# Turns in the interleaving of two graph layers on TensorE: hysteresis beside the MLP, and another course

## The chip, the cores and the metric

The kernel runs on one core of a Trainium2 chip. The metric is the device time of the program in microseconds. TensorE is called PE in the profile (its weight loads PEld), VectorE DVE, ScalarE ACT, GpSimd POOL, SyncE SP.

## The reference

Two graph layers follow each other on 16 images of 1024 nodes with 256 features, in float32. Layer 0 is a graph attention with four heads of 64 features; in the inputs the adjacency is 0 or 1, so of its five edge types only one occurs. Layer 1 is a masked self-attention with eight heads of 32 features, and an MLP from 256 to 1024 to 256 features with GELU. A layer norm closes each of them.

```python
# layer 0 (type 1 alone, since adj is 0 or 1)
h = einsum('bnd,hde->bhne', x, W)
weight = leaky_relu(mask * (e_src[i] + e_dst[j]), 0.01)      # e_* = h . a_*
att = softmax(where(adj == 0, -1e9, weight))
out = relu(att @ h + bias) + h                               # per head, then a norm per head
x = layernorm(x + out)
# layer 1
n = layer_norm(x) ; q = k = v = heads of n
attn = softmax(where(adj > 0, q @ k.T / sqrt(32), -inf))
x = x + attn @ v
x = layernorm(x + gelu(layer_norm(x) @ W1 + b1) @ W2 + b2)
```

## The kernel before

All code in question is in `fast_path`; `general_path` runs only when a check of the inputs fails. The program is written out instruction by instruction in Python, and the order in which the Python calls are made is the order on TensorE, ScalarE, VectorE and GpSimd. There is no loop on the device: all 16 images are unrolled.

Two generators issue the heavy work. `layer0()` goes image by image through `prepare` (transposes, projections, the mask) and `attention0`; `layer1()` goes through `attention1` and `mlp` one image behind. Each `yield` ends a step, and gives the step's size in units of estimated TensorE time and what the next step needs.

- An `attention0` step, 1.0 unit, is one pair of key blocks for one head and 512 queries. `products` issues 16 matmuls (32 records, since a float32 matmul shows as two) in array tiles of 128*64 from the weights tile `p0` into the PSUM bank `acc`. `weights` makes the `p0` of the step three later (`AHEAD = 3`, four buffers) with two VectorE instructions. There are 32 such steps in an image. Every 16 of them `spread_factor` puts four 32*128 matmuls between.
- An `attention1` step, 2.5 units, has four row-tiled logit matmuls (`ps`, a ring of four PSUM banks), four exponentials on ScalarE, two mask products on VectorE, and value products in tiles of 128*32 (`po`). There are 32 in an image, and they take 82 to 83 units with their beginning.
- An `mlp` step, 1.75 units, is two hidden blocks of the first product (`first`: `ps<-yT,w_sb`, then GELU on ScalarE), or half of one output block of the second (`second`: `po<-w_sb,hid`). Either way it is 8 records in tiles of 128*128. There are 32 in an image, 56 units.

Besides there are `chains`, generators of the smaller work that follows a step: norms, residuals, transposes. `advance()`, which is called after each step, issues a chain's next part as soon as the planner's clock (`Pace`, a model of engine times) has its inputs ready.

The main loop picks the stream of the next step. `place` holds the image and the units done of each stream. `wanted()` turns layer 1's progress into the place where layer 0 should be, along `COURSE`: `WORK0` is 13 + 2 + 32 = 47 units, `ATTN1` 82, `WORK1` 138. Layer 0 has the turn when it is behind the target. A second rule swaps the two when the chosen stream's inputs come over 0.3 us later by the planner's clock than the other's, within `SLACK` of the target:

```python
    SLACK = 0.06
    COURSE = [(0.0, 1.0), (ATTN1, 1.38), (WORK1 - 14.0, 2.0), (WORK1, 2.0)]
    ...
        which = 0 if streams[0] and (at0 < target or not streams[1]) else 1
        if all(streams):
            late = [when(n) - nc.now() for n in needs]
            other = 1 - which
            allowed = at0 < min(target + SLACK, place[1][0] + 2.05) if other == 0 else at0 > target - SLACK
            if allowed and late[which] > max(late[other], 0.0) + 0.3:
                which = other
```

`COURSE` says that layer 0 of image b+1 is to have 38% of its 47 units done when layer 1's attention of image b ends, and all of them 14 units before the MLP of image b ends.

Of the kernel before, what the change touches and what calls it, by code (L numbers as in the profile page):

```python
# [176 lines left out]
def fast_path(  # L177
# [141 lines left out]
    def at_time(t):  # L319
        return lambda: t  # L320
# [94 lines left out]
    def when(needs):  # L415
        return max([n() if callable(n) else nc.written.get(n.tensor.name, 0.0) for n in needs] + [0.0])
# [18 lines left out]
    def begin(chain, engine, *needs):  # L435
        for n in needs:
            if not callable(n):
                uses(chain, n.tensor.name)
        chains.append([chain, engine, needs])
# [10 lines left out]
    def advance():  # L450
        for _ in range(2):
            for item in list(chains):
                if item in chains and when(item[2]) <= max(nc.now(), nc.free[item[1]]):
                    run(item)
# [4 lines left out]
    def done(chain):  # L459
        return lambda: math.inf if waits(chain) else 0.0  # L460

    def complete(chain):

        for item in list(chains):
            if item[0] is chain:
                while item in chains:
                    run(item)
# [366 lines left out]
    def finish1(o, x1, yT, heads):  # L834


        complete(heads)
        rowwise = [P, BPH, D]
        nc.vector.tensor_add(o, o, x1)
        mv = small.tile([P, BPH, 2], F32, name="mv1")  # L840
        for g in range(BPH):
            statistics(o[:, g, :], mv[:, g, :])
        v = small.tile([P, BPH], F32, name="v1s")
        nc.vector.tensor_scalar(v, mv[:, :, 1], EPS, None, op0=OP.add)
        r = power(v, BPH, "r1")
        nc.vector.tensor_add(x1, x1, o)
        yield "vector", r
        t = minus_mean(mv[:, :, 0], r, BPH)
        yield "scalar", t
        scale_shift(o, o, t, r, BPH)  # L850
        for g in range(0, BPH, GB):
            yield "tensor", o, side_ready
            transpose_rows(yT[:, :, g * P : (g + GB) * P], o[:, g : g + GB, :])

    def add_bias2(x1):
        nc.vector.tensor_add(x1, x1, b2_r[:, None, :].to_broadcast([P, BPH, D]))
        yield from ()

    def in_range(values):

        for op, bound in ((OP.max, LOW), (OP.min, HIGH)):
            seen = small.tile([P, NR], F32, name="seen")
            nc.vector.scalar_tensor_tensor(seen, values, bound, values, op0=op, op1=OP.is_equal)
            nc.vector.tensor_tensor(okr, okr, seen, op=OP.min)
# [78 lines left out]
    def finish_norms(b, n):  # L943
        for chain in [c for at, c in norms.items() if at[:2] == (b, n)]:
            complete(chain)

    place = [[0, 0.0], [0, 0.0]]

    def layer0():
        for b in range(B):  # L950
            place[0][:] = b, 0.0
            seen = three.tile([P, NR], F32, name="ranges")
            rinv1 = seen[:, 0 : NB * H1].rearrange("p (k h) -> p k h", h=H1)
            rinv0 = seen[:, NB * H1 : NB * (H1 + H0)].rearrange("p (k h) -> p k h", h=H0)
            factors = seen[:, NB * (H1 + H0) : NR].rearrange("p (k h) -> p k h", h=H0)
            hb = []
            esr = one.tile([P, N], F32, name="esr")
            dinv = two.tile([P, NB, H0], F32, name="dinv")
            v0 = one.tile([P, NB, H0, HO + 1], F32, name="v0")
            mask = [two.tile([P, NB, HALF], U8, name=f"mask{n}") for n in range(NH)]  # L960
            yield from prepare(b, hb, esr, v0, dinv, mask)
            handed[b] = seen, rinv1, mask
            yield from attention0(b, hb, v0, esr, dinv, factors, mask, rinv0)
        place[0][:] = B, 0.0

    def layer1():
        for b in range(B):
            place[1][:] = b, 0.0
            seen, rinv1, mask = handed.pop(b)

            def half(n):
                if (b, n) not in handed:
                    finish_norms(b, n)
                return handed[b, n]

            yT = [two.tile([P, DC, HALF], F32, name="yT") for _ in range(NH)]
            halves = {}

            def half_done(n, o, heads):
                finish_norms(b, n)  # L980
                x1 = handed[b, n][0]
                chain = finish1(o, x1, yT[n], heads)
                bias = add_bias2(x1)
                halves[n] = x1, yT[n], chain, bias
                begin(chain, "vector", done(heads), o)
                begin(bias, "vector", at_time(nc.now() + 24.0), x1)

            yield from attention1(half, mask, rinv1, half_done)
            complete(weights_of_later)
            yield from mlp(b, halves)  # L990
            in_range(seen)
# [4 lines left out]
    WORK0 = NB // GB * 3.25 + 2.0 + NB * H0 * 1.0  # L996
    ATTN1 = 2.0 + 2.5 * (NH * NB * H1 // QUAD)
    WORK1 = ATTN1 + NB // GB * (1.75 * FC / 2 + 3.5 * GB)
    SLACK = 0.06
    COURSE = [(0.0, 1.0), (ATTN1, 1.38), (WORK1 - 14.0, 2.0), (WORK1, 2.0)]  # L1000

    def wanted():
        b, done = place[1]
        for (start, low), (end, high) in zip(COURSE, COURSE[1:]):
            if done < end:
                return b + low + (high - low) * (done - start) / (end - start)
        return b + COURSE[-1][1]

# [2 lines left out]
    load_blocks(0)  # L1011
    weights_of_later = later_weights()
    begin(weights_of_later, "tensor", at_time(3.0))
    streams, needs = [layer0(), layer1()], [(), ()]
    while any(streams):
        (b0, done0), target = place[0], wanted()
        at0 = b0 + done0 / WORK0
        which = 0 if streams[0] and (at0 < target or not streams[1]) else 1
        if all(streams):
            late = [when(n) - nc.now() for n in needs]  # L1020
            other = 1 - which
# [3 lines that stand above are left out]
        step = next(streams[which], None)  # L1025
        if step is None:
            streams[which], needs[which] = None, ()
        else:
            place[which][1] += step[0]
            needs[which] = step[1:]  # L1030
        advance()
# [393 lines left out]
@with_exitstack  # L1425
def tile_two_graph_layers(ctx: ExitStack, tc: tile.TileContext, *args: bass.AP):
    nc = tc.nc
    pool = ctx.enter_context(tc.tile_pool(name="outcome", bufs=1))
    ok = pool.tile([P, 1], F32, name="ok")
    fast_path(tc, *args, ok)  # L1430
    verdict = pool.tile([1, 1], I32, name="verdict")
    with tc.tile_pool(name="ps_v", bufs=1, space=PSUM) as ps_v, tc.tile_pool(name="sb_v", bufs=1) as sb_v:
        ident = sb_v.tile([P, P], F32, name="ident_v")
        make_identity(nc, ident)
        row = ps_v.tile([1, P], F32, name="row")
        nc.tensor.transpose(row, ok, ident)
        least = sb_v.tile([1, 1], F32, name="least")
        nc.vector.tensor_reduce(least, row, axis=mybir.AxisListType.X, op=OP.min)
        nc.vector.tensor_copy(verdict, least)
    good = nc.values_load(  # L1440
        verdict[0:1, 0:1], min_val=0, max_val=1, skip_runtime_bounds_check_because="it is a product of comparisons"
    )
    with tc.If(good == 0):
        general_path(tc, *args)
# [34 lines left out]
```

## Time and profile before

| what | value |
|---|---|
| time, median of 3 runs | 3568.07 us (3567.42 to 3569.54) |
| the profiled execution | 3565.24 us, its span 3563.4 us |
| granted TensorE clock | 0.974 over the span |
| busy over the span | PE 3446.7, DVE 2984.4, ACT 2010.3, POOL 416.4 us |
| layer 0's products (`acc<-v,p`) | 16384 records, 585.7 us busy, 227 ns each |
| MLP products (`ps<-yT,w_sb` and `po<-w_sb,hid`) | 2048 records each, 487.1 and 490.6 us busy, 386 and 387 ns each |
| one image in the middle of the run | 217.2 us (1847.9 to 2065.1 us) |

Nearly all instructions stand under L61, the line of a helper, so groups are told apart by tile names. The ends of matmuls are modelled and their pipeline overlaps, so for TensorE the difference between the starts of two neighbouring groups says more than the mean duration of one instruction. A line of the timeline merges neighbouring instructions of one form; its count divided by 32 (layer 0's products) or by 8 (the MLP) is a number of steps.

### The profile page before, as it was taken

What the parts mean: (1) busy time and instruction counts of PE and PEld (TensorE: products, weight loads), DVE (VectorE), ACT (ScalarE), POOL (GpSimd) and SP (SyncE); (2) the same over time, 40 slices, a digit from 0 to 9 for tenths busy, and PEclk for the clock granted to TensorE, in tenths of its full rate; (3) what the DMA queues carried; (4) which work ended last, traced back from release to release, by engine and by line L of the source; (5) the groups of instructions that cost most, each with busy time, mean ns of one, the idle gap of its engine ahead of it and who ended that gap; (6) DMA issues with size and microseconds to landing.
All of it is one profiled execution on the core that took longest, in us unless ns stands there. A gap on an engine that the chain in (4) does not pass through costs nothing.

```text
span 3563.4 us, 141495 instructions
## 1 busy us (share of the span) xinstructions
PE 3446.7 (97%) x64417; PEld 2301.0 (65%) x64417; DVE 2984.4 (84%) x5267; ACT 2010.3 (56%) x4320; POOL 416.4 (12%) x424
## 2 busy tenths in 40 slices
PE   6899999999999999999999999999999999999998
PEld 5567576675756658576575766757567585765746
DVE  5898897988879898898988979889798988979873
ACT  2563736547375573846638366473755738466363
POOL 0102011010110101111020110101101011110200
PEclk8899999999999999999999999999999999999999
DMA  4101102011020110201011020110201102010000
GB/s 107 38 15 34 30 13 48 8 36 27 15 48 6 40 21 16 47 12 41 15 32 32 13 45 9 34 30 14 49 6 40 21 15 48 12 37 3 18 4 14
DMA packets 77811, 97.52 MB, mean 27 GB/s; under 512 B 9105, under 2 KB 60049, under 8 KB 77201
## 3 DMA queue, kind: packets, MB, share of 16 engines
q0 software_dynamic: 18432, 33.56, 6.5%
q1 hardware_dynamic: 57184, 53.76, 4.9%
q8 instruction: 506, 8.29, 1.0%
q10 hardware_dynamic: 1584, 1.05, 0.1%
q14 instruction: 105, 0.85, 0.1%
HBM read 105.13 MB, written 16.78 MB: 34 GB/s over the span
## 4 chain that ended last, share of the span: by engine, by line
PE 84%; DVE 8%; ACT 4%; issue 2%; DMA 1%; POOL 0%; POOLq 0%; ACTq 0%; DVEq 0%
PE po L61 32%; PE ps L61 31%; PE acc L61 22%; DVE p L61 7%; ACT p L61 2%; ACT sq L61 1%; DVE x L61 1%; ACT mask L61 1%; ACT z L61 0%; DMA w0e<-in_L_gnn_W_dram 0%; DVE hb L61 0%; ACT oT L61 0%; DMA xl<-in_L_gnn_a_dst_dram 0%; ACT o L61 0%; ACT xT L61 0%
## 5 line engine op out<-in xcount | busy, mean ns | idle before, releaser
L61 ACT ACTIVATE p<-ps 128x512 f32<-128x512 f32 x2048 | 1059.6, 610 | 388.2 <-PE ps L61 388.2
L61 DVE TENSOR_TENSOR p<-p,mask 128x1024 f32<-128x1024 f32 x1024 | 1187.6, 1216 | 13.1 <-ACT p L61 13.1
L61 PE MATMUL ps<-nT 32*128 32x512 f32 x4096 | 715.5, 666 | 1.5 <-ACT p L61 1.5
L61 DVE SCALAR_TENSOR_TENSOR p<-cb,dinv,mask 128x512 f32<-128x512 f32 x1024 | 710.9, 743 | 0.7 <-ACT cb L61 0.7
L61 PEld LDWEIGHTS acc<-v,p 128*64 128x64 f32 x16384 | 525.1, 140 | 129.2 <-issue 68.4
L61 PE MATMUL acc<-v,p 128*64 128x65 f32 x16384 | 585.7, 227 | 19.9 <-DVE p L61 12.3
L61 PEld LDWEIGHTS po<-v,p 128*32 128x32 f32 x32768 | 393.0, 110 | 327.7 <-issue 305.9
L61 ACT ACTIVATE hid<-ps,b_sb 128x256 f32<-128x256 f32 x512 | 242.6, 474 | 632.8 <-PE ps L61 632.8
L61 PE MATMUL po<-p,unit 128*32 128x512 f32 x2048 | 550.6, 612 | 0.0
L61 PE MATMUL po<-p,v 128*32 128x512 f32 x2048 | 550.2, 612 | 0.3 <-issue 0.3
L61 PE MATMUL po<-w_sb,hid 128*128 128x256 f32 x2048 | 490.6, 387 | 0.0
L61 PE MATMUL ps<-yT,w_sb 128*128 128x256 f32 x2048 | 487.1, 386 | 0.0
L61 PEld LDWEIGHTS ps<-yT,w_sb 128*128 128x128 f32 x2048 | 376.6, 190 | 64.7 <-issue 11.4
L61 PEld LDWEIGHTS po<-w_sb,hid 128*128 128x128 f32 x2048 | 375.6, 190 | 65.1 <-issue 11.4
L61 PE MATMUL po<-v,p 128*32 128x33 f32 x32768 | 386.8, 198 | 12.1 <-DVE o L61 10.2
L61 PEld LDWEIGHTS ps<-nT 32*128 32x128 f32 x4096 | 241.9, 190 | 121.5 <-issue 50.6
L61 PEld LDWEIGHTS po<-p,v 128*32 128x32 f32 x2048 | 78.3, 108 | 343.9 <-issue 183.2
L61 DVE TENSOR_TENSOR z<-acc,bias_r 128x256 f32<-128x256 f32 x128 | 54.3, 424 | 249.4 <-ACT hb L61 249.2
L61 POOL TENSOR_TENSOR r<-v,mhalf 128x1 f32<-128x1 f32 (+1 forms) x192 | 156.5, 824 | 775.3 <-DVE v L61 631.0
L61 ACT COPY cb<-ps 128x512 f32<-128x512 f32 x128 | 68.8, 589 | 254.7 <-PE ps L61 254.7
L61 POOL TENSOR_TENSOR r<-v1s,mhalf 128x4 f32<-128x4 f32 x32 | 61.6, 1925 | 1078.2 <-DVE v1s L61 1078.2
L61 POOL DMA_DIRECT2D ak<-in_adj_dram x128 | 69.0, 539 | 917.1 <-PE acc L61 897.5
(109 smaller groups left out, 2989.8 us busy)
## 6 DMA issues: line engine op xcount, KB each, us to landing
ak<-in_adj_dram POOLq DMA_DIRECT2D x128, 256.0 KB, 3.9
xk<-in_x_dram SPq DMA_DIRECT2D x64, 256.0 KB, 2.8
xl<-in_x_dram SPq DMA_DIRECT2D x32, 512.0 KB, 3.9
out_dram<-z SPq DMA_DIRECT2D x128, 128.0 KB, 1.7
w_sb<-in_L_gnn_W_dram SPq DMA_DIRECT2D x2, 1024.0 KB, 6.6
v<-in_L_gnn_a_src_dram SPq DMA_DIRECT2D x2, 320.0 KB, 4.4
v<-in_L_gnn_a_dst_dram ACTq DMA_DIRECT2D x1, 320.0 KB, 7.0
xl<-in_L_gnn_a_dst_dram ACTq DMA_DIRECT2D x1, 320.0 KB, 8.2
```

Source lines behind the costliest of these rows:

```text
L61: return method(*args, **kwargs)
```

## The change

It adds a hysteresis to the rule that picks the stream: while layer 1 is in its MLP, the stream that had the last step is favoured by `STAY` = 0.018 of layer 0's course. `which` is kept from one round to the next for that, and it is the stream that really had the step, after the rule on lateness. The course now asks for 34% of layer 0 instead of 38% at the end of layer 1's attention, and lateness may move the place by 0.08 instead of 0.06.

```diff
-    SLACK = 0.06
-    COURSE = [(0.0, 1.0), (ATTN1, 1.38), (WORK1 - 14.0, 2.0), (WORK1, 2.0)]
+    SLACK = 0.08
+    STAY = 0.018
+    COURSE = [(0.0, 1.0), (ATTN1, 1.34), (WORK1 - 14.0, 2.0), (WORK1, 2.0)]
...
-    streams, needs = [layer0(), layer1()], [(), ()]
+    streams, needs, which = [layer0(), layer1()], [(), ()], 0
...
-        which = 0 if streams[0] and (at0 < target or not streams[1]) else 1
+        stay = 0.0 if place[1][1] < ATTN1 else (STAY if which == 0 else -STAY)
+        which = 0 if streams[0] and (at0 < target + stay or not streams[1]) else 1
```

## The prediction

> **What bounds the kernel now.** I read the page first, then the sums over stretches of one image, then TensorE's timeline in the stretch that the change touches, then what one tile's matmuls wait for. From the page, busy time by engine:
>
> ```profile
> PE 3446.7 (97%) x64417; PEld 2301.0 (65%) x64417; DVE 2984.4 (84%) x5267; ACT 2010.3 (56%) x4320; POOL 416.4 (12%) x424
> ```
>
> TensorE is never free for long, so a gain must come from what its busy time is made of. An image takes about 217 us (one image's last MLP turn starts at 1847.9 us, the next one's at 2065.1). Three stretches of it, TensorE first, VectorE third:
>
> ```profile
> 1721.00:1770.70 49.70, 49.01 (x1346) 27.91 (x1345) 48.97 (x67) 30.45 (x59) 1.94 (x1) 1.00 0.02 4
> 1770.70:1847.90 77.20, 77.20 (x1027) 63.60 (x1025) 65.84 (x145) 26.12 (x54) 14.19 (x11) 1.00 0.05 17
> 1847.90:1860.20 12.30, 12.30 (x62) 10.57 (x60) 10.47 (x25) 4.19 (x7) 3.10 (x3) 1.00 0.12 30
> ```
>
> The first is the end of layer 1's attention with the first steps of the next image's layer 0 attention between; VectorE works 48.97 of 49.70 us there. The second is the MLP with layer 0's attention beside it: TensorE 77.20 of 77.20 us, VectorE 65.84. The third is the end of the MLP alone. The granted clock is 1.00 in all. In the second, layer 0's products never wait (the tile view of `acc`; nothing stands under the third line):
>
> ```profile
> L61 PE MATMUL acc<-v,p x800: 220/222/271, 1776.0 to 1847.7; 128*64 128x65 f32 x160
> its engine sat idle before it (us, times) until:
> who waited for it (us, times):
> ```
>
> So the MLP stretch is bound by TensorE's own instruction stream. TensorE's timeline there (start, duration, tile shape of the array, operands, count), the usual pattern and then the one place with longer turns:
>
> ```profile
> 2000.11 1.15 PE L61 MATMUL acc<-v,p 128*64 128x65 f32 x32
> 2001.19 1.99 PE L61 MATMUL po<-w_sb,hid 128*128 128x256 f32 x8
> 2003.11 1.15 PE L61 MATMUL acc<-v,p 128*64 128x65 f32 x32
> 2004.20 1.99 PE L61 MATMUL po<-w_sb,hid 128*128 128x256 f32 x8
> 2006.12 2.09 PE L61 MATMUL acc<-v,p 128*64 128x65 f32 x64
> 2008.14 1.13 PE L61 MATMUL ps<-esr,spread 32*128 32x512 f32 x4
> ```
>
> ```profile
> 1837.19 3.02 PE L61 MATMUL acc<-v,p 128*64 128x65 f32 x96
> 1840.14 1.99 PE L61 MATMUL po<-w_sb,hid 128*128 128x256 f32 x8
> 1841.97 1.89 PE L61 MATMUL ps<-yT,w_sb 128*128 128x256 f32 x8
> 1843.80 1.15 PE L61 MATMUL acc<-v,p 128*64 128x65 f32 x32
> 1844.88 1.99 PE L61 MATMUL po<-w_sb,hid 128*128 128x256 f32 x8
> ```
>
> One layer 0 step is 32 matmul records, one MLP step 8. Take differences of starts, since the ends are modelled. A lone layer 0 step holds TensorE 1.08 us (2000.11 to 2001.19), two 2.02 (2006.12 to 2008.14), three 2.95 (1837.19 to 1840.14): 0.93 a step, and 0.15 each time the stream comes on. A lone MLP step holds it 1.92 us (2001.19 to 2003.11), two 3.66 (1840.14 to 1843.80): every join saves 0.2. **A pair of changes, there and back, costs 0.35 us.** Counted in the timeline from 1770.7 to 1860.2 us, the MLP's 32 steps stand in 21 turns, 16 of them one after another of a single step, with 25 layer 0 steps in 20 turns between.
>
> [...] 1792.6 to 1813 us of VectorE's timeline show `p` pairs of 1.41 us set between row-wise operations of up to 1.22 us.
>
> **The change, part by part.** No instruction is added or removed, no buffer changes, and each stream keeps its order; only the interleaving moves. The order of TensorE, ACT, DVE and POOL is the order in which the program is written. The DMAs of the moved steps are the loads of `xl` (512 KB, in the norms that follow layer 0's products) and the stores of `z`, on SP, past each other by a few us; landing takes 3.9 and 1.7 us by the page. POOL's adjacency loads belong to layer 0's preparation, beside layer 1's attention. No matmul in the MLP stretch waits for a DMA, so I put nothing on them; were that cover gone, one landing would be the cost.
>
> *STAY.* One layer 0 unit is 1/47 of the course. The old rule takes layer 0 whenever it is behind the target. Now the stream that ran last has 0.018 x 47 = 0.85 units of credit, so a turn ends after the position has crossed a band of 1.7 units. An MLP step moves the target by 1.75 x 0.66/42 x 47 = 1.29 units: a turn takes two MLP steps, sometimes three, and then two or three of layer 0. I stepped both rules by hand with unit steps and without the rule on lateness. Old, from 22 units at 83 of layer 1's: 3 MLP steps, then single ones, 22 turns and 25 layer 0 steps. The trace has 21 and 25 with the same beginning, so the stepping can be trusted. New, from 21 units: 4, then 2 or 3, at the end 9 alone, 11 turns. Ten pairs of changes fall away: 10 x 0.35 = 3.5 us an image. The lateness rule (line 1023) can swap streams inside a turn, now within 0.08. In the trace it altered one place of 21; VectorE will be tighter, so I allow for 1.5 broken turns: **-8.5 x 0.35 = -3.0 us** (ends -3.5 and -2.1).
>
> *COURSE and SLACK.* The last step that lateness allows before the MLP starts was that from 21 units (21/47 = 0.447, under 0.395 + 0.06); now that from 20 (0.426 under 0.356 + 0.08; 0.447 is over it). One layer 0 step of seven leaves layer 1's attention for the MLP, where it costs 0.93 us. What leaves is 1.08 us if TensorE is the bound there. It is only about 0.45 us if the step hid the exponentials: an attention step takes 2.63 us at best (1725.94 to 1728.57) and 3.25 with no filler before the next (1728.57 to 1731.82), against 2.63 + 1.08 with one. And it is 1.41 us if VectorE bounds there, which its 48.97 of 49.70 us speak for. Ends +0.5 and -0.5 us; I take 0.
>
> *Work that gets between.* In the stretch four groups of transposes or factor spreads stand where the streams change over, which costs little. With turns of two and two to three, some two of five step borders lie inside a layer 0 turn: 4 x 0.4 x 0.35 = **+0.55 us** (ends 0 and 1.4).
>
> *A new wait.* A turn of three asks for three `p` pairs in 2.8 us, and VectorE makes one in 1.41. The cover is the three pairs made ahead (AHEAD) in four buffers; they fill while two MLP steps run (3.66 us). Behind a late pair on TensorE stands all of both streams, and then VectorE's own norms. VectorE idles 7.8 us of the 77.2 (summed gaps in the trace). The stretch loses about 2.5 us and gains 1.4 of work, so some 4 us of slack are left. The trace has no such turns in number, so bounds: nothing, or 0.35 us in each of 10 turns, 3.5 us. I take **+0.6**.
>
> Sum: -3.0 + 0 + 0.55 + 0.6 = -1.85 us an image. Fifteen images have a partner (15 closing MLP turns; the last MLP runs alone, and the first layer 0 too): **-28 us**. The profiled execution took 3565.24 us (span 3563.4): 3537 for it. The median of the three runs is 2.8 us above it: 3540 us.
>
> **Rivals.** (a) Everything falls away and nothing waits: 15 x (3.5 + 0.2 - 0.3) = 51 us, 3517. For it: the acc view without a wait. Against: VectorE's load. Chance 0.2.
> (b) Lateness breaks the turns, so that the change hardly does what it says: the planner's own VectorE is nearly full too, a third `p` of a turn is seen 0.3 us late, and the stream swaps. Two or three pairs saved are eaten by the other terms: 3560 to 3570. The 16 single steps in a row without a swap speak against it. Chance 0.1.
> (c) Slower: VectorE becomes the bound of the MLP stretch. If a turn starts with one pair ready, its second and third step each wait 1.41 - 0.93 = 0.48 us; in half of ten turns that is 4.8 us an image against 2.4 saved: +2.4 x 15 = +36 us, 3604. It decides from 0.24 us of wait per turn. For it: 92% of the stretch is VectorE's once the saving is made[...]. Against: the turn of three at 1837.19 ran in 2.95 us without a wait. Chance 0.1.
>
> **How the numbers follow.** The forecast has 0.6, and spans -45 to -12 us. A measurement here tells about 0.2%, 7 us, from no change. Faster: 0.6 + 0.2 and a little of (b), 0.82; same: most of (b), 0.08; slower: (c), 0.10. The range 3512 to 3562 holds the forecast and (a) and leaves out (c) and the greater part of (b).
>
> **What would show it.** Right: in the MLP stretch 8-record groups come as 16 or 24 and 32-record groups as 64 or 96, about 11 to 13 MLP turns an image; a lone closing turn of up to nine; an image of about 215.3 us; the stretch still without waits of `acc`; `acc` and MLP matmuls of the same mean duration. Wrong: waits "PE acc <- DVE p" of tens of us (12.3 us in the whole run now) would mean (c); more than 17 turns an image would mean (b); a longer stretch 1721 to 1770.7 would put the fault in the course, not in the turns.

## The result, and the profile after

The changed kernel takes 3509.26 us (median of four runs, 3502.05 to 3519.75) against 3568.81 for the kernel before: ratio 0.9835, interval 0.9808 to 0.9862. A second series gave 3501.26 against 3567.57, ratio 0.9813 (0.9799 to 0.9826). It is faster by 59 to 66 us. The forecast was faster by 28, and 3509 lies just below its range of 3512 to 3562.

The page after, first line of busy time, and the core's span with its mean granted clock, before and after:

```profile
PE 3388.7 (97%) x64417; PEld 2288.7 (65%) x64417; DVE 2983.8 (85%) x5267; ACT 2005.7 (57%) x4320; POOL 424.0 (12%) x424
```

```profile
core 0: 3563.4 us, clock 0.974
```

```profile
core 0: 3510.3 us, clock 0.981
```

TensorE has as many matmuls as before, and VectorE and ScalarE work as long; TensorE is busy 58 us less. The second pair of lines holds what the prediction did not look at. (1 - 0.974) x 3563.4 is 93 us that the clock took away before, (1 - 0.981) x 3510.3 only 67 after.

Two stretches of one image follow: the whole MLP, and the opening of layer 1's attention up to its first value products. The columns are PE, PEld, DVE, ACT and POOL busy with counts, the granted clock and the DMA. First before, then after:

```profile
1770.70:1860.17 89.47, 89.47 (x1083) 74.15 (x1081) 76.29 (x170) 30.31 (x61) 17.29 (x14) 1.00 0.06 19
1860.17:1875.77 15.60, 13.31 (x65) 6.92 (x64) 11.03 (x29) 13.85 (x31) 3.58 (x5) 0.81 0.40 88
```

```profile
1742.90:1831.57 88.67, 88.67 (x1126) 76.11 (x1125) 76.03 (x166) 31.78 (x64) 17.78 (x14) 1.00 0.09 23
1831.57:1844.74 13.17, 11.38 (x58) 5.71 (x57) 10.89 (x31) 12.01 (x32) 3.59 (x5) 0.87 0.33 80
```

The whole MLP, where the turns are, is only 0.8 us shorter, with a 26th layer 0 step and two pieces of the next image's preparation in it. The opening of this image is 2.4 us shorter; ScalarE is busy for 89 and 91% of it, and the clock stands at 0.81 and 0.87. The forecast did not look at this place.

The turns themselves look as forecast (TensorE's timeline after; 96 records are three layer 0 steps, 16 two MLP steps):

```profile
1776.40 3.02 PE L61 MATMUL acc<-v,p 128*64 128x65 f32 x96
1779.35 1.99 PE L61 MATMUL ps<-yT,w_sb 128*128 128x256 f32 x8
1781.18 3.62 PE L61 MATMUL po<-w_sb,hid 128*128 128x256 f32 x16
1784.73 2.09 PE L61 MATMUL acc<-v,p 128*64 128x65 f32 x64
1786.75 1.13 PE L61 MATMUL ps<-esr,spread 32*128 32x512 f32 x4
1787.80 1.15 PE L61 MATMUL acc<-v,p 128*64 128x65 f32 x32
```

Three layer 0 steps still hold TensorE 2.95 us, and the last three lines show a factor spread that now splits a turn of layer 0. In every image the MLP stands in 12 turns instead of 21, and the streams change over 22 times instead of 40; 11 to 13 turns were forecast. The wait for `p`, from the waits of TensorE after, is what it was over the whole run:

```profile
PE acc L61 <- DVE p L61: 12.3, 8, 3.1
```

What did not stand in the prediction is the end of the MLP (timeline of TensorE, before and after):

```profile
1853.17 7.07 PE L61 MATMUL po<-w_sb,hid 128*128 128x256 f32 x32
1860.17 1.14 PE L61 MATMUL ps<-nT 32*128 32x512 f32 x8
1861.24 0.66 PE L61 MATMUL acc<-ident,xk 128*128 128x128 f32 x4
```

```profile
1820.76 1.15 PE L61 MATMUL acc<-v,p 128*64 128x65 f32 x32
1821.85 0.66 PE L61 MATMUL ps<-ident,xk 128*128 128x128 f32 x4
1822.34 0.61 PE L61 MATMUL acc<-identb,ak 128*128 128x128 bf16 x8
1822.79 1.95 PE L61 MATMUL ps<-yT,w_sb 128*128 128x256 f32 x8
1824.57 7.07 PE L61 MATMUL po<-w_sb,hid 128*128 128x256 f32 x32
1831.57 1.14 PE L61 MATMUL ps<-nT 32*128 32x512 f32 x8
```

After layer 0's last step of the image now stand the first two pieces of the next image's preparation: the transposes of x (`xk`) and those of one mask block (`ak`). Before, they came after the first logits of the attention (`ps<-nT`), at 1861.24 us. The rule that the diff adds does this: layer 0 has just had its turn, so its credit of 0.018 is added, and its place 2.0 is below 2.0 + 0.018. The two pieces are 0.95 units, 0.020 of the course, and then the place is past it. I call them the pulled pieces.

### The profile page after: what moved, and what is told of

The parts are those of the page before. It is cut to its first block, busy times and chain, and to the rows that moved or that the text cites. A ratio compares the mean times of both kernels' runs of the same rounds, so it can differ in the third digit from the quotient of the medians.

```text
span 3510.3 us, 141526 instructions
## 1 busy us (share of the span) xinstructions
PE 3388.7 (97%) x64417; PEld 2288.7 (65%) x64417; DVE 2983.8 (85%) x5267; ACT 2005.7 (57%) x4320; POOL 424.0 (12%) x424
## 4 chain that ended last, share of the span: by engine, by line
PE 83%; DVE 9%; ACT 6%; issue 2%; DMA 0%; POOL 0%; ACTq 0%; POOLq 0%; DVEq 0%
PE po L61 32%; PE ps L61 30%; PE acc L61 20%; DVE p L61 7%; ACT p L61 2%; ACT sq L61 1%; DVE x L61 1%; ACT mask L61 1%; ACT hb L61 0%; ACT oT L61 0%; ACT z L61 0%; DMA w0e<-in_L_gnn_W_dram 0%; DVE hb L61 0%; DVE z L61 0%; ACT v L61 0%
## 5 line engine op out<-in xcount | busy, mean ns | idle before, releaser
L61 PE MATMUL ps<-nT 32*128 32x512 f32 x4096 | 698.7, 653 | 0.9 <-ACT p L61 0.7
L61 PEld LDWEIGHTS acc<-v,p 128*64 128x64 f32 x16384 | 514.6, 140 | 99.6 <-issue 48.8
L61 PE MATMUL acc<-v,p 128*64 128x65 f32 x16384 | 558.8, 226 | 19.4 <-DVE p L61 12.3
L61 PE MATMUL po<-w_sb,hid 128*128 128x256 f32 x2048 | 465.9, 381 | 0.0
L61 PEld LDWEIGHTS po<-w_sb,hid 128*128 128x128 f32 x2048 | 387.1, 190 | 63.3 <-issue 11.4
L61 PEld LDWEIGHTS ps<-nT 32*128 32x128 f32 x4096 | 233.4, 187 | 120.9 <-issue 44.8
L61 POOL TENSOR_TENSOR r<-v,mhalf 128x1 f32<-128x1 f32 (+1 forms) x192 | 163.8, 861 | 564.1 <-DVE v L61 529.3
L61 PE MATMUL acc<-w0e,xT 128*128 128x264 f32 x512 | 157.8, 433 | 37.7 <-DVE z L61 22.6
L61 POOL TENSOR_TENSOR r<-v0s,mhalf 128x8 f32<-128x8 f32 x64 | 129.1, 2017 | 526.4 <-DVE v0s L61 526.4
```

Of the source, the lines that this page charges most:

```text
L61: return method(*args, **kwargs)
```

## The experiments

Each run is against the kernel before in the same series (medians 3567.57, 3567.0, 3566.59 and 3569.06 us). "Lost clock" is span times one minus the mean granted clock, median over a kernel's runs. The stretches are means over 14 images of the one profiled execution, read from the trace: MLP; opening, from here on from the first logits to the seventh group of value products, some 36 us; what the clock took from the opening; rest of the attention. The profiled execution is seldom the median one: that of `no_pull` and that of `after_again` are 21 us apart, the medians 32.

| kernel | time | ratio (interval) | lost clock | MLP | opening | its lost clock | rest |
|---|---|---|---|---|---|---|---|
| before | 3567.6 | | 89 | 89.4 | 36.9 | 4.0 | 90.6 |
| course_only | 3562.5 | 0.9986 (0.9979, 0.9992) | 89 | 90.6 | 37.2 | 4.3 | 89.0 |
| no_pull | 3533.3 | 0.9894 (0.9876, 0.9912) | 74 | 87.7 | 37.3 | 3.0 | 89.5 |
| pull_first | 3522.7 | 0.9883 (0.9866, 0.9900) | 74 | 88.1 | 36.6 | 2.7 | 88.8 |
| after_again | 3501.3 | 0.9813 (0.9799, 0.9826) | 60 | 88.6 | 35.6 | 2.7 | 88.9 |
| pull_only | 3548.7 | 0.9950 (0.9936, 0.9964) | 64 | 90.3 | 35.4 | 2.3 | 90.1 |
| stay_only | 3564.9 | 0.9997 (0.9989, 1.0004) | 96 | 89.2 | 37.2 | 3.9 | 90.0 |
| stay_cap | 3510.2 | 0.9834 (0.9820, 0.9847) | 60 | 87.9 | 35.4 | 2.4 | 90.1 |
| act_light | 3477.6 | 0.9749 (0.9736, 0.9762) | 35 | 87.7 | 34.1 | 0.6 | 89.4 |
| sq_dve | 3501.4 | 0.9814 (0.9800, 0.9827) | 60 | 88.6 | 34.9 | 1.8 | 89.0 |
| pull_more | 3525.7 | 0.9881 (0.9864, 0.9899) | 74 | 90.0 | 35.6 | 3.0 | 88.7 |
| pull_far | 3584.6 | 1.0053 (1.0040, 1.0067) | 93 | 99.2 | 30.6 | 4.8 | 88.7 |
| stay_long | 3603.0 | 1.0099 (1.0084, 1.0115) | 104 | 86.6 | 43.8 | 4.8 | 88.9 |
| early | 3645.0 | 1.0220 (1.0206, 1.0234) | 98 | 103.0 | 33.9 | 0.0 | 85.1 |
| long_early | 3644.0 | 1.0215 (1.0201, 1.0229) | 109 | 103.0 | 33.9 | 0.0 | 85.1 |
| slack06 | 3690.2 | 1.0342 (1.0328, 1.0357) | 136 | 104.9 | 35.0 | 1.7 | 85.1 |
| early_hold | 3565.1 | 0.9993 (0.9985, 1.0002) | 43 | 97.4 | 34.5 | 0.7 | 85.0 |

**Taking the change apart.** `no_pull` keeps turns and course, and keeps the pulled pieces out:

```diff
-        stay = 0.0 if place[1][1] < ATTN1 else (STAY if which == 0 else -STAY)
+        stay = 0.0 if place[1][1] < ATTN1 or at0 > place[1][0] + 1.99 else (STAY if which == 0 else -STAY)
```

> The changed kernel, but the credit STAY no longer counts once layer 0 has finished its image, so that the next image's first transposes (x and mask of block 0) stay out of the end of the MLP. Turns and course stay as in the changed kernel (13 MLP turns, 26 layer 0 steps beside the MLP). Theory P (the unforeseen half of the gain comes from these two pieces being pulled into the MLP[...]): lost clock rises from 68 us to about 90 us, the time to 3533 (3525 to 3545) us. Rival T (the whole gain comes from the turns and the moved step): 3509, within 8 us. Rival L[...]: lost clock scatters, no steady difference to the changed kernel.

3533.3 us, as theory P said. Its lost clock did not rise to 90 but to 74, so clock alone is not the link.

`pull_only` is the kernel before with the pulled pieces alone (`STAY` is 0.018, and `which` is kept, as in the change):

```diff
-        which = 0 if streams[0] and (at0 < target or not streams[1]) else 1
+        stay = STAY if place[1][1] >= ATTN1 and which == 0 and at0 > place[1][0] + 1.99 else 0.0
+        which = 0 if streams[0] and (at0 < target + stay or not streams[1]) else 1
```

> The kernel before, with its course, slack and single turns (21 MLP turns, 25 layer 0 steps), but the next image's first two pieces of preparation go ahead of the last seven MLP steps. Theory P: lost clock falls from 92 us towards 68 us, the time to 3543 (3533 to 3553) us. Rival T: 3568, within 5 us. Rival L: 3568 with more scatter than before.

3548.7 us, 19 us faster, with the old turns. The pieces cost the MLP 0.9 us and save the rest of the image more. T and L fall: all five runs lie below all 25 of the kernel before.

`course_only` has `stay = 0.0`:

> The changed kernel without STAY: course 1.34 and slack 0.08 alone, 6 layer 0 steps beside layer 1's attention and 26 beside the MLP, turns mostly single, nothing pulled. Theory P with the prediction's term of nothing for the moved step: attention stage shorter by some 1.1 us an image, MLP stage longer by about as much, 3567 (3558 to 3575) us. Rival C (the attention stage was bound by VectorE and loses 2.7 us an image by the course alone): 3528 to 3545 us.

3562.5 us, 5 us faster. The moved layer 0 step costs the MLP 1.1 us and takes 1.5 from the attention after the opening. C falls.

> The changed kernel once more, beside the others on the same chip: 3500 to 3520 us, lost clock 55 to 75 us. Under rival L its scatter would reach the time of the kernel without the pulled pieces; under P it stays below it.

3501.3 us. So in this series the change of -66 us is course -5, turns -29 (course_only to no_pull), pulled pieces -32 (no_pull to the changed kernel). The last part is the least certain: the five runs of `no_pull` go from 3519 to 3534 us, and the nine of the changed kernel in both series from 3500 to 3520.

`pull_first` lets only the first piece through (credit 0.005 at the image's end):

> The changed kernel with the credit at the image's end cut to 0.005, so that only the first of the two pieces (x transposes and their copy, 0.6 us of ScalarE) goes into the end of the MLP; the mask piece (1.3 us of ScalarE) stays at the start of layer 1's attention. Turns as in the changed kernel. Theory A (the opening of the attention is bound by ScalarE, so the gain goes with the ScalarE work taken out): one third of the gain, 3524 (3516 to 3530) us. Rival K[...]: all or nothing, so 3502 or 3533, with lost clock to match.

3522.7 us, a third of the gain, as A said, but its runs lie from 3512 to 3533 with lost clock from 63 to 81: this run excludes neither A nor K, by which the gain is lost clock alone.

**What bounds the opening.** `act_light` is `no_pull` with less work in two ScalarE instructions. It leaves TensorE's and ScalarE's order alone, and leaves out seven of eight column blocks of two masks, so its output isn't the reference's:

```diff
+            if b >= 3 and k < GB:
+                nc.enter("scalar", "activation", (dst, pt, AF.Square), rest)
+                nc.nc.gpsimd.memset(dst[:, 1:NB, :], 1.0)
+                nc.nc.scalar.activation(dst[:, 0:1, :], pt[:, 0:1, :], AF.Square, **rest)
```

> The kernel without the pulled pieces (13 turns, 3533 us), with the same order on TensorE, VectorE and ScalarE; but in images 3 to 15 the first two mask activations of the preparation (1.1 to 1.2 us of ScalarE each, both in the opening of layer 1's attention) handle one of their eight column blocks, and a GpSimd memset fills the other seven, so these masks are wrong. Some 0.8 us less of ScalarE each, 1.6 us an opening. Theory A (ScalarE bounds the opening): the opening falls by about 1.6 us in 13 images, 21 us: 3512 (3503 to 3520) us. Rival K (the opening is bound by TensorE and its cold clock, ScalarE follows): 3533, within 8 us.

3477.6 us: 56 us less, where A alone said 21. One opening of `no_pull`, then one of `act_light` (sums up to the first value products):

```profile
1839.12:1855.40 16.28, 14.57 (x73) 7.88 (x76) 12.82 (x32) 15.12 (x37) 3.72 (x5) 0.91 0.44 98
```

```profile
1819.19:1832.60 13.41, 12.44 (x73) 7.01 (x76) 11.39 (x31) 12.26 (x35) 5.29 (x7) 1.00 0.55 119
```

ScalarE is busy 93% of the first and 91% of the second. With its two activations shorter this stretch is 2.9 us shorter, and the clock is 1.00 instead of 0.91. Lost clock falls from 74 to 35 us. K falls. Work on ScalarE holds TensorE up here (its wait for `mask` in the opening falls from 1.4 to 0.7 us). What brings the clock down was not shown.

How much is clock can be read from images whose openings lost the same. Take the whole attention, from the first logits to the MLP. Where the opening lost 3.41 us, it takes 126.9 us before (mean of 9 images) and 125.7 in `pull_only` (6), 127.2 in `no_pull` (9) and 125.8 in `after_again` (6). So at an equal clock the pulled pieces save 1.2 to 1.4 us there, of which the MLP takes 0.9 back. Where nothing was lost, `no_pull` takes 124.7 us (2 images) and `act_light` 123.0 (11): 1.7 us, close to A's 1.6. The rest of both gains goes with the clock. Why the clock loss falls with the pulled pieces was not shown. TensorE's recorded waits do not fall: 35.2 us for `mask` before, and in the changed kernel 38.8 us for `z`, by which VectorE reads the same PSUM banks out (waits of TensorE, before and after):

```profile
PE acc L61 <- ACT mask L61: 35.2, 17, 2.3
```

```profile
PE acc L61 <- DVE z L61: 38.8, 36, 1.6
```

`sq_dve` moves 2.1 us of ScalarE to VectorE instead (the changed kernel, four `scalar.activation` of the second half's norm as `vector.tensor_scalar`):

> The changed kernel, but the normalising of the second half of layer 0's output (four ScalarE instructions, 2.1 us, in the opening of layer 1's attention) is done by VectorE. Turns and pulled pieces as in the changed kernel; nothing is left out. Theory A (ScalarE bounds the opening, and each microsecond off it also spares cold clock): the opening falls by 1 to 2 us, 3480 (3465 to 3492) us. Rival K: 3505, within 8 us. Rival V (VectorE takes over as the bound of the opening): 3510 to 3530 us.

3501.4 us, the changed kernel's time. TensorE's waits for `z` are as long as there, 39.8 us against 38.8. What changed is who is full. One opening up to the first value products:

```profile
1827.90:1842.32 14.42, 11.99 (x63) 6.39 (x63) 13.90 (x43) 11.67 (x30) 3.69 (x5) 0.88 0.37 91
```

VectorE is busy 96% of it, where it was 83% in the changed kernel's opening (10.89 of 13.17 us), and ScalarE 81% instead of 91%. So the opening has little slack on VectorE either, and A holds only where the work isn't handed to VectorE.

**More pulled pieces, and STAY alone.** `pull_far` raises the course's end to 2.12 and the cap to 2.15:

> The changed kernel, but the course rises to 2.12 at the end of the MLP and the cap to 2.15: eight or nine pieces of the next image's preparation go between the last five MLP steps instead of two pieces ahead of them. Theory A: some 5 us more of ScalarE work leave the opening, which falls by 2 to 4 us an image while the MLP grows by the pieces' own TensorE time: 3480 (3465 to 3495) us. Rival S (these pieces only change places, or wait in the MLP for the norms on VectorE): 3500 to 3515 us.

3584.6 us: the opening falls by 5.0 us from the changed kernel's, but the MLP grows by 10.5. Missed by both theories. Of the 10.5 us only 2.8 are waits of TensorE for VectorE (`z`, in the image from 1785 to 1877 us); the rest is TensorE's own work that moved, and 2 us of what the opening gained goes to the clock (4.8 us lost in it instead of 2.7).

`pull_more` has `(WORK1, 2.045)` in the course:

> The changed kernel with the course at 2.045 at the MLP's end: two more pieces (a projection and a mask, some 2 us of ScalarE) go before the last MLP step. Theory A, if their ScalarE work ends before the first exponentials: 3490 (3480 to 3500) us. If it stands in the way of the first exponentials, as with STAY alone: the first exponential comes 1 to 3 us later, 3510 to 3535 us.

3525.7 us; the MLP grows by 1.4 us, the opening does not fall. The reading offered for a loss, a later first exponential, is wrong: it comes 1.16 us into the opening, as in the kernel before.

`stay_only` has STAY with the old course and slack:

> STAY alone, with the course 1.38 and the slack 0.06 of before: 14 MLP turns, 7 and 25 layer 0 steps, the two pieces pulled ahead of the last seven MLP steps and two more pieces after them. Additive theory: turns -28 us, pull -22 us or more, course nothing: 3515 (3503 to 3525) us. Rival C (the turns need the new course, which frees VectorE beside the attention): 3530 to 3550 us.

3564.9 us, no gain. The additive theory missed by 50 us. Its opening starts at 1853.1 us, and ScalarE's timeline shows what comes before the first exponentials (`p<-ps`; lines left out are marked):

```profile
1852.96 1.28 ACT L61 ACT_TABLE_LOAD   x1
...
1854.63 1.14 ACT L61 ACTIVATE mask<-acc,shift_c 128x1024 uint8<-128x1024 bf16 x1
...
1855.73 2.08 ACT L61 ACTIVATE sq<-hb,t,r 128x256 f32<-128x256 f32 x4
...
1858.68 2.05 ACT L61 ACTIVATE p<-ps 128x512 f32<-128x512 f32 x4
```

Two further pieces had come in at the MLP's very end. A table load of 1.28 us, a mask of 1.14 and a norm of 2.08 stand in ScalarE's queue, and the first exponential comes 5.6 us into the opening instead of 1.2. `stay_cap` takes those two pieces away alone (cap 2.015 instead of 2.05):

> STAY alone with course 1.38 and slack 0.06, and a cap of 2.015 instead of 2.05, so that just the two pieces are pulled, ahead of the last seven MLP steps, and the two that followed them (their ScalarE work stood before the first exponentials) stay behind. If those two pieces are why STAY alone gave nothing: 3520 (3508 to 3530) us, first exponential 1.2 us into the opening instead of 5.6. Rival C (the turns need the new course): 3545 to 3565 us.

3510.2 us, a ratio of 0.9834 against 0.9813. Turns and two pulled pieces give nearly the whole gain under the old course too; C falls.

**Longer turns, other courses.** `stay_long` has STAY 0.04:

> The changed kernel with STAY 0.04 instead of 0.018: the program has 11 MLP turns an image, layer 0 turns of up to five steps, 7 layer 0 steps beside layer 1's attention and no pulled piece. Theory W (0.35 us a pair of changes, and no new wait): two pairs fewer than the kernel without the pulled pieces, one step back in the attention: 3528 (3520 to 3536) us, waits of layer 0's products for p as before, some 12 us in all. Rival V (turns of four and five outrun VectorE, 1.41 us a p pair against 0.93 us a step): waits of 0.5 to 1.5 us in each long turn, 3540 to 3570 us.

3603.0 us, but neither theory: its MLP is the shortest of all at 86.6 us. A turn of five steps runs in 4.82 us (1817.15 to 1821.97), and `acc` waits for nothing in the MLP:

```profile
1817.15 4.89 PE L61 MATMUL acc<-v,p 128*64 128x65 f32 x160
1821.97 1.35 PE L61 MATMUL ps<-yT,w_sb 128*128 128x256 f32 x5
```

The loss is in the opening, 43.8 us: layer 0's last step now comes after the MLP, inside the opening, and the chain of norms that starts from that step keeps the attention waiting. TensorE's waits for `z` grow from 38.8 us in the changed kernel, those for `sq` from 2.9:

```profile
PE acc L61 <- DVE z L61: 61.8, 36, 3.7
PE acc L61 <- ACT sq L61: 44.8, 16, 7.4
```

`early` has slack 0.06 and the course at 2.0 already 17.5 units before the end, `long_early` STAY 0.03 besides, `slack06` the changed kernel with slack 0.06. All three have 3 layer 0 steps beside the attention instead of 6, and 29 beside the MLP.

> The changed kernel with slack 0.06 and the course at 2.0 already 17.5 units ahead of the MLP's end: 3 layer 0 steps beside the attention and 29 beside the MLP in turns of two and three, the two pieces pulled, then ten MLP steps alone. Theory A: layer 0 ends some 8 us earlier, so its norms are over before the opening, which gets no longer than in the changed kernel; the three steps moved gain what the course run gave (0.35 us each): 3490 (3480 to 3502) us. Rival F (three steps less beside the attention leave exponentials uncovered, 3.25 us a step instead of 2.63): the attention stage does not fall by the 1.1 us a step that the MLP grows by, 3510 to 3530 us.

> The one before with STAY 0.03: turns mostly of three and four, about 11 MLP turns an image, 3 steps beside the attention, two pieces pulled, ten MLP steps alone at the end. If the switch price of 0.35 us a pair holds in turns of four and VectorE keeps up, it stands 8 to 15 us below the run with 0.018 of the same course, at 3478 (3465 to 3492) us. Rival V (VectorE is outrun): above it, with waits for p.

> The changed kernel with the slack 0.06 of before instead of 0.08: 3 layer 0 steps beside the attention instead of 6, 29 beside the MLP, turns of two and three at first and single ones at the end, two pieces pulled, six MLP steps alone. If turns and opening are what counts: about two turns more than the changed kernel, +10 us, the opening the same: 3512 (3503 to 3525) us. If the three moved steps matter by VectorE's load in the attention: 3490 to 3500 us.

3645.0, 3644.0 and 3690.2 us; every expectation missed. Their attention is 4 to 5.5 us shorter than the changed kernel's, their MLP 14 to 16 longer. In `early` three moved steps are some 3 of the 14 us, lost clock inside the MLP is 4.3 (none in the changed kernel), and a new wait is 6.6. That wait among TensorE's waits in `early`, and VectorE's timeline at the start of its MLP:

```profile
PE acc L61 <- DVE relu L61: 104.1, 16, 6.6
```

```profile
1802.39 1.22 DVE L61 TENSOR_TENSOR o<-o,x 128x1024 f32<-128x1024 f32 x1
...
1805.99 1.22 DVE L61 TENSOR_TENSOR x<-x,o 128x1024 f32<-128x1024 f32 x1
1807.12 1.41 DVE L61 SCALAR_TENSOR_TENSOR p<-cb,dinv,mask 128x512 f32<-128x512 f32 x2
...
1808.73 0.42 DVE L61 SCALAR_TENSOR_TENSOR relu<-acc,ranges 128x256 f32<-128x256 f32 x1
```

A head of layer 0 ends just there. The next step's matmuls wait until that head's residual (`relu`) has been read out of its bank, and this read stands in VectorE's order behind the norm of layer 1's second half: 6.6 us, in which TensorE does neither stream. `early_hold` keeps layer 0 out of the last attention step and the first six MLP steps:

> The early course (3645 us) with layer 0 held back during the first six MLP steps, so that its head's last products no longer come while layer 1's norm fills VectorE. Turns are shorter after that, some 17 MLP turns. If the wait for the residual behind that norm is the cause (6.6 us in each of 15 images[...]): the wait goes, MLP stretch about 92 us instead of 103, 3540 (3520 to 3560) us. Rival F (the three steps that left the attention are the loss): 3620 to 3650 us.

3565.1 us, 80 us less than `early`. The waits for `relu` fall from 104 to 18.6 us in all, and lost clock from 98 to 43. The MLP is still 97.4 us, not 92: it has 16 turns instead of 12, and what else it holds was not taken apart. F falls for the greater part of the loss.

## Why the prediction was right or wrong

**The switch price held.** From `course_only` to `no_pull` the change-overs fall from 40 to 22 an image, nine pairs, and the MLP by 2.8 us: 0.31 us a pair, with the splits by the spreads in it. The prediction had 3.0 us for the turns and gave 1.15 of it back.

**The new wait did not come.** The +0.6 us for late `p` was 0, up to turns of five. What works against long turns is elsewhere.

**The moved step** was taken at 0 within half a microsecond: 1.1 us more in the MLP, 1.5 less in the rest of the attention, 0.3 more in the opening.

**The sum was near for what it covered, in part by luck.** Course and turns together are -34 us where it said -28. The turns gave 2.8 us an image in the MLP, against 1.85 in the sum. But the attention behind them grew by 0.6 us (126.2 to 126.8, from `course_only` to `no_pull`), a term that the sum did not have.

**The step that failed** is the end of the stepping, "at the end 9 alone", and the sum that stops there. I stepped the rule only up to the end of layer 0's image. One step further it says that layer 0, having had the last turn, is credited into the next image; the hand stepping itself gives one piece ahead of the nine (2.0 is under the target of 1.988 + 0.018). In the trace layer 0 ends four MLP steps later, where the target is 2.0, and two pieces go ahead of the last five MLP steps. The prediction said "only the interleaving moves", and it priced no move of the preparation and nothing in the opening behind the MLP: it showed three stretches with the clock at 1.00, and left out the fourth, at 0.81. The runs put there what the forecast lacked: without the pulled pieces 3533 us, inside the stated range, with them 3501, so -32 us (-19 in the kernel before).

**Rivals.** (a) came near in size for another reason: its 51 us were to be turns alone. (b) did not occur. (c), VectorE as the bound with waits for `p`, did not occur, but another course shows its kin: in `early` waits for `relu` behind a norm in VectorE's order cost TensorE 104 us.

## What to carry to other kernels

When a change moves the interleaving of two streams, follow the rule across the border of a period, and price the place where the streams meet, not only the stretch that the change names. Read the granted clock of every stretch: where it is below 1.00, a small move can come out larger than it is (it was 0.91 in an opening of `no_pull`, where 21 us less of ScalarE work, in `act_light`, gave 56). In the full stretch the savings came near to what was counted (0.31 us a pair of changes against 0.35); what a freed or delayed chain met at the border made the difference between 66 us faster and 123 us slower.

## What the runs showed of the hardware

In the traces of the kernel before and the changed kernel, openings of some 36 us lost from 1.71 to 5.12 us to the clock. Of the first 14 openings of the changed kernel six lost 1.71 us, seven 3.41 and one 5.12; of those before nine lost 3.41 us and five 5.12. In the changed kernel's opening at 1831.57 us the granted clock was 0.50 from 1837.37 to 1840.78 us, and 1.00 before and after that. The changed kernel's runs lie 18 us apart in the first series and 8 in the second: the fastest and the slowest lost 56 and 74 us in the first, 63 and 67 in the second.

Lost clock was not lost time one for one. Over the 21 runs of `course_only` the time rises by some 0.4 us for each us of lost clock, over the 21 of `stay_only` by 0.8. Where the opening lost 3.41 us instead of 1.71, the attention was 2.7 us longer in the changed kernel's first series (126.0 against 123.3), 2.6 in `after_again` and only 0.3 in `pull_only`.
